# Dividing layer 0's softmax rows before the turn, a token-tile last step in layer 2, and one pool of tiles

## The chip, the cores and the metric

One core of one Trainium2 chip. The metric is device time in microseconds (us), the median of the runs. The kernel before takes 4326.4 us (4324.36 to 4327.26); the prediction starts from 4325.7 us, one of these runs. Runs of one kernel agree within 0.2%, so differences of 10 us are read as real where three rounds were timed.

## The reference, cut to what matters

64 graphs of 256 nodes with 256 features pass through four layers, each added to its input after a layer norm and a ReLU. Only layers 0 and 2 change.

```python
# layer 0: 8 heads of 32, masked softmax over keys
scores = einsum('bhqd,bhkd->bhqk', q, k) / sqrt(32)
w = softmax(where(adj > 0, scores, -1e9), axis=-1)
ctx = einsum('bhqk,bhkd->bhqd', w, v)            # then @ Wo + bo
# layer 2: three GRU steps, the adjacency passing messages
for i in range(3):
    aggr = einsum('bst,bsd->btd', A, h @ weight[i])
    r = sigmoid(i_r + h_r); z = sigmoid(i_z + h_z)
    n = tanh(i_n + r * h_n)
    h = (1 - z) * n + z * h
```

Layer 1 is a graph attention, layer 3 one with four heads.

## The kernel before

Two graphs make a pair, 32 pairs in all. Every piece of work is a task: one or more forms (engine, assumed duration, instructions), what it reads, writes and claims. A list scheduler in the kernel orders all tasks beforehand from the assumed durations, picking at each step the task and form that can begin first. The result is one fixed queue for each engine; on the chip each queue runs strictly in that order.

```python
def evict(n, dst, src):                      # an eviction: copy a result out of PSUM; either engine may do it
    return [(A, act(n), lambda: nc.scalar.copy(dst(), src())),
            (V, dve(n), lambda: nc.vector.tensor_copy(dst(), src()))]
def dve2(n):
    return 0.065 + n / 1920.0
def pool(n):
    return 0.16 + n / 460.0

SLOTS = {...
    "w4": (20, [P, T * D], FP, 6),           # count, shape, type, reserve for the oldest pair
    "w8": (4, [P, 8, N], FP, 1),
    "w2": (5, [P, N2], FP, 2), "rzw": (4, [P, 2, 4, D0], FP, 2), ...}
```

In layer 0 the exponentials of a row are turned (transposed on TensorE) undivided. The reciprocals of the row sums are widened to 32 columns a head, turned as well, and multiply the context.

```python
add(exp_group(s, mx, zs, rows, ...), reads=[(mx, half)], writes=[s, (zs, half)])
for k in range(2):
    add((PE, 4 * TURN, turn), reads=[s], writes=[ps], claims=[pT[half]])
    add(evict(N2, ...), reads=[ps], writes=[(pT[half], (ti, k))])
# ... after both tiles of the graph:
add((V, 0.2, reciprocal(rz, zs)));  add((V, 0.22, copy(rzw, rz widened)))
add((PE, 4 * TURN, turn_rz), reads=rzws, writes=[psz])      # four transposes
add((A, act(N2), copy(rzT, psz)))
add((PE, 1.93, context), ...)
add((V, dve(N2), cT = psc * rzT))
```

In layer 2 each gate is computed with features along the partitions, so that its bias rides on ScalarE's activation; each step ends with eight transposes back to tokens.

```python
ps = gate(3.44, ((whhT, hT), (giT[:, l], aT)), o * P, o)     # 4 fp32 products of 512 columns
add((A, act(N2, 1), tanh(r, ps, bias=brz[:, o:o+1], scale=0.5)))
# ... u = 0.5 * (z' + 1) * (h - n) + n
add((PE, 4 * TURN, tokens), reads=[hT], writes=[ps])          # twice
add_to_x(xt, g, ps)                                           # last step: VectorE, out of PSUM
```

## Time and profile before

| | kernel before |
|---|---|
| median | 4326.4 us |
| TensorE, VectorE, ScalarE, GpSimd busy | 98%, 68%, 53%, 14% |
| one pair of graphs, in the periodic part | 132.47 us |

How the page and the start distances are read stands in the prediction. What TensorE waited for between 1000 and 4200 us (total, times, longest) is little:

```profile
PE ps L930 <- ACT w L401: 8.7, 8, 1.1
PE ps L909 <- DVE w L402: 5.7, 7, 0.8
PE ps L840 <- DVE w L828: 4.7, 8, 0.6
```

GpSimd's timeline during the slow VectorE group that the prediction shows (2065.72 us, 3.62 us for four operations):

```profile
2065.04 1.27 POOL L811 TENSOR_TENSOR w<-w,w 128x512 f32<-128x512 f32 x1 [9.81 <-ACT w L806]
2066.64 1.27 POOL L811 TENSOR_TENSOR w<-w,w 128x512 f32<-128x512 f32 x1 [0.32 <-ACT w L806]
2067.88 1.31 POOL L506 TENSOR_TENSOR x<-x,bo_bc 128x512 f32<-128x512 f32 x1
2069.41 1.75 POOL L506 TENSOR_TENSOR x<-x,bo_bc 128x512 f32<-128x512 f32 x1 [0.23 <-DVE w L445]
```

### The profile page before, as it was taken

Reading aid. Unit: us, or ns where it says so; the run is one execution under the profiler, and the core shown is the slowest. Engines: PE = TensorE matmul, PEld = TensorE weight load, DVE = VectorE, ACT = ScalarE, POOL = GpSimd, SP = SyncE. Lnnn points to the kernel's source line nnn. Section 1 sums busy time; section 2 is a strip of 40 time slices with the busy share of each in tenths; the row PEclk is TensorE's granted clock in tenths of the full one; section 3 lists DMA queues with packets and bytes.
Section 4 is the critical chain, followed back from the end, with each engine's and each line's share of the span. In section 5 each row is a group of like instructions: output and inputs, shape, how many; then the busy total and the mean of one; then the engine's idle time right before and its main releaser. Section 6 shows DMA issues by size and latency. Waiting matters only on the chain.

```text
span 4324.5 us, 56216 instructions
## 1 busy us (share of the span) xinstructions
PE 4244.1 (98%) x20720; PEld 2631.3 (61%) x20720; DVE 2930.0 (68%) x5426; ACT 2301.1 (53%) x6105; POOL 590.3 (14%) x582
## 2 busy tenths in 40 slices
PE   7999999999999999999999999999999999999997
PEld 5665566656656665666566566656655665666564
DVE  6775577667657755876676577558765765776554
ACT  4664465545545644655455456446554554564444
POOL 1111111111111111111111111111111111111111
PEclk9999999999999999999999999999999999999999
DMA  2000011000000000010000000000100100000000
GB/s 83 21 18 22 20 36 34 20 16 24 30 25 25 13 28 25 30 35 20 11 30 30 25 25 13 27 25 26 40 11 17 32 30 25 25 13 28 15 15 15
DMA packets 109986, 108.47 MB, mean 25 GB/s; under 512 B 7312, under 2 KB 109712, under 8 KB 109712
## 3 DMA queue, kind: packets, MB, share of 16 engines
q1 hardware_dynamic: 109712, 104.89, 7.6%
q8 instruction: 163, 2.67, 0.3%
q14 instruction: 111, 0.91, 0.1%
HBM read 88.09 MB, written 16.78 MB: 24 GB/s over the span
## 4 chain that ended last, share of the span: by engine, by line
PE 77%; DVE 8%; issue 8%; ACT 5%; POOL 1%; SPq 0%; DMA 0%; POOLq 0%; ACTq 0%; DVEq 0%
PE ps L761 36%; PE ps L775 7%; PE ps L518 5%; PE ps L480 5%; PE ps L573 4%; PE ps L717 3%; PE ps L654 3%; PE ps L540 2%; PE ps L457 2%; PE ps L614 2%; PE ps L840 2%; PE ps L858 2%; ACT w L886 2%; ACT w L494 2%; DVE w L823 1%
## 5 line engine op out<-in xcount | busy, mean ns | idle before, releaser
L761 PE MATMUL ps<-w,whhT 128*128 128x512 f32 x2304 | 1080.3, 595 | 0.7 <-DVE w L402 0.4
L761 PE MATMUL ps<-w,giT 128*128 128x512 f32 x2304 | 1063.6, 593 | 0.0
L494 ACT ACTIVATE w<-w,mx 128x256 f32<-128x256 f32 x1664 | 825.7, 503 | 186.3 <-DVE mx L561 128.9
L401 ACT COPY w<-ps 128x512 f32<-128x512 f32 x983 | 553.0, 587 | 657.3 <-PE ps L775 290.8
L761 PEld LDWEIGHTS ps<-w,giT 128*128 128x128 f32 x2304 | 433.6, 190 | 523.9 <-issue 513.3
L761 PEld LDWEIGHTS ps<-w,whhT 128*128 128x128 f32 x2304 | 415.3, 190 | 406.6 <-issue 383.9
L811 POOL TENSOR_TENSOR w<-w,w 128x512 f32<-128x512 f32 x192 | 251.2, 1317 | 1689.6 <-ACT w L806 1331.8
L402 DVE COPY w<-ps 128x512 f32<-128x512 f32 x553 | 366.4, 684 | 153.7 <-PE ps L573 58.0
L786 ACT ACTIVATE w<-ps,brz 128x512 f32<-128x512 f32 x192 | 131.8, 687 | 463.2 <-PE ps L761 460.3
L791 DVE TENSOR_SCALAR w<-w 128x512 f32<-128x512 f32 x192 | 81.6, 425 | 407.8 <-ACT w L786 407.7
L554 DVE SCALAR_TENSOR_TENSOR w<-ps,mask 128x512 f32<-128x512 f32 x512 | 333.3, 680 | 33.9 <-PE ps L540 33.9
L775 PE MATMUL ps<-w,w 128*128 128x256 f32 x1536 | 355.7, 379 | 0.0
L775 PEld LDWEIGHTS ps<-w,w 128*128 128x128 f32 x1536 | 286.2, 190 | 60.7 <-issue 22.9
L494 ACT ACTIVATION_READ_ACCUMULATOR w<-w,mx 128x1 f32 x1664 | 322.9, 194 | 0.0
L823 DVE SCALAR_TENSOR_TENSOR w<-w,w 128x512 f32<-128x512 f32 x192 | 152.5, 794 | 246.3 <-ACT w L818 240.7
L561 DVE TENSOR_REDUCE mx<-w 128x4 f32<-128x1024 f32 x256 | 309.2, 1208 | 2.0
L573 PE MATMUL ps<-ident,w 128*128 128x128 f32 x2048 | 269.4, 273 | 0.6
L573 PEld LDWEIGHTS ps<-ident,w 128*128 128x128 f32 x2048 | 235.1, 140 | 57.1 <-issue 25.6
L818 ACT ACTIVATE w<-ps,brz 128x512 f32<-128x512 f32 x192 | 130.8, 681 | 235.0 <-PE ps L761 234.9
L424 POOL TENSOR_SCALAR rs<-mv 128x4 f32<-128x4 f32 x128 | 33.6, 262 | 1354.8 <-DVE mv L417 1293.5
L886 ACT ACTIVATE w<-w,f 128x256 f32<-128x256 f32 x512 | 217.1, 503 | 1.4
L445 DVE TENSOR_SCALAR w<-x,mv,rs 128x256 f32<-128x256 f32 x384 | 185.3, 541 | 16.5 <-POOL rs L425 15.8
(113 smaller groups left out, 5633.0 us busy)
## 6 DMA issues: line engine op xcount, KB each, us to landing
adj<-in_adj_dram SPq DMA_DIRECT2D x128, 512.0 KB, 4.1
x<-in_x_dram SPq DMA_DIRECT2D x64, 256.0 KB, 2.8
out_dram<-x SPq DMA_DIRECT2D x64, 256.0 KB, 2.2
gg_sb<-in_L_gnn_weight_dram SPq DMA_DIRECT2D x3, 256.0 KB, 3.7
wih_sb<-in_L_gnn_w_ih_dram SPq DMA_DIRECT2D x1, 768.0 KB, 6.9
whh_sb<-in_L_gnn_w_hh_dram SPq DMA_DIRECT2D x1, 768.0 KB, 8.6
wq_sb<-in_L_gnn_Wq_dram SPq DMA_DIRECT2D x1, 256.0 KB, 2.8
wk_sb<-in_L_gnn_Wk_dram SPq DMA_DIRECT2D x1, 256.0 KB, 3.0
```

What stands on the lines that cost most here:

```text
L401: (A, act(n), lambda: nc.scalar.copy(dst(), src())),
L402: (V, dve(n), lambda: nc.vector.tensor_copy(dst(), src())),
L480: mm(ps()[:, c * D : (c + 1) * D], chunk(src, k, 2 * g + c), rhs[:, k, :], start=k == 0, stop=k == 1)
L494: nc.scalar.activation(tok(e(), N)[:, i, :], tok(e(), N)[:, i, :], AF.Exp, bias=mx()[:, m : m + 1], accum_out=zs()[:, z : z + 1],)
L518: mm(ps(), w[:, k, o * P : (o + 1) * P], tok(hT(), N2)[:, k, :], start=k == 0, stop=k == 1)
L554: (V, dve(N2), lambda s=s, j=j, b=b, t=t: nc.vector.scalar_tensor_tensor(tok(s(), N)[:, 2 * j : 2 * j + 2, :], tok(b(), N), SCALE, tok(mb( ...
L561: (V, dve(4 * N), lambda s=s, mx=mx, h4=h4: nc.vector.tensor_reduce(mx()[:, h4], tok(s(), N), AX.X, ALU.max, negate=True)),
L573: nc.tensor.transpose(tok(ps(), P)[:, 2 * i + c, :], tok(s(), N)[:, 2 * k + i, c * P : (c + 1) * P], ident,)
L761: mm(ps(), w[:, k, c0 : c0 + P], at_o(src, k), start=n == 0, stop=n == 2 * len(terms) - 1)
L775: mm(ps()[:, g * N : (g + 1) * N], tok(h())[:, t, o * P : (o + 1) * P], tok(am(), N)[:, t, :], start=c == 0, stop=c == 1,)
L811: (G, pool(N2), lambda o=o, u=u, hT=hT, hn=hn: nc.gpsimd.tensor_sub(at_o(u, o), at_o(hT, o), at_o(hn, o))),
L886: (A, act(N, 1), lambda t=t, g=g, h=h, e=e: nc.scalar.activation(tok(e(), N)[:, h, :], tok(sd[h // 2](), N2)[:, h % 2, g * N : (g + 1) * N ...
```

## The change

The intent is to take transposes off TensorE, the busiest engine: the row division moves ahead of the turn, so the reciprocals need no turn of their own; layer 2's last step gives token tiles (tokens along the partitions) at once. The tiles of 8 KB become pairs of 4 KB from one pool.

```diff
-        "w4": (20, [P, T * D], FP, 6),
-        "w8": (4, [P, 8, N], FP, 1),
+        "w4": (28, [P, T * D], FP, 9),
-        "w2": (5, [P, N2], FP, 2),
+        "w2": (4, [P, N2], FP, 2),
-        "rzw": (4, [P, 2, 4, D0], FP, 2),
+    row_bcast(brz_bc, b_ih[0:N2])          # and bhn_bc, bhh_bc: biases along the free axis
# layer 0, per tile and half
+    add((V, 0.13, rz = 1 / zs), reads=[(zs, half)], writes=[(rz, half)])
     for k in range(2):
+        add([(V, 2 * dve2(N), divided),     # two tensor_scalar of 128x256 with a pointer scalar
+             (G, pool(N2), lambda ...: nc.gpsimd.tensor_tensor(two(), two(),
+                 rz()[:, z0 : z0 + 2].unsqueeze(2).to_broadcast([P, 2, N]), ALU.mult))],
+            reads=[(rz, half)], writes=[(s, k)])
-        add((PE, 4 * TURN, turn), reads=[s], writes=[ps], claims=[pT[half]])
+        add((PE, 4 * TURN, turn), reads=[(s, k)], writes=[ps], claims=[pT[2 * half + k]])
-    add((V, 0.22, widen rz)); add((PE, 4 * TURN, turn_rz)); add((A, act(N2), copy rzT))
-    add((V, dve(N2), cT = psc * rzT))
+    add(evict(N2, cT, psc))
# layer 2, last step: token chunks stationary, weights moving
+    add((PE, 3.44, tokens_mm(ps, both, t, 0, N2)))                      # r and z of a chunk
+    add((V, dve(N2), rz[g] = ps + brz_bc)); add((A, act(N2), tanh(rz[g], scale=0.5)))
+    add((V, ..., hn = (r + 1) * hn)); add((V, ..., hn = 0.5 * hn + ps))
+    add((V, ..., hn += bias));        add((A, act(N2), tanh(hn)))
+    add((G, pool(N2), h = h - hn));   add((G, pool(N2), x = x + hn))
+    add((V, ..., h = (z + 1) * h));   add((V, ..., x = 0.5 * h + x))
-    add((PE, 4 * TURN, tokens)); add_to_x(xt, g, ps)                    # last step only
# ... cut: layer 3's eT from the same pool, the moved helper for the messages
```

More of the change, by code (lines that the diff above doesn't have):

```diff
@@ L266, in tile_adj_preln_d4 @@
     nc.sync.dma_start(bhh_sb, b_hh.rearrange("(k p) -> p k", p=P))
+    brz_bc = const.tile([P, N2], FP, name="brz_bc")
+    bhn_bc = const.tile([P, 2, D], FP, name="bhn_bc")
+    row_bcast(brz_bc, b_ih[0:N2])
+    row_bcast(bhn_bc[:, 0], b_ih[N2 : 3 * D])
+    row_bcast(bhn_bc[:, 1], b_hh[N2 : 3 * D])
     with tc.tile_pool(name="prep", bufs=1) as prep:
@@ L283, in transposed @@
                     nc.vector.tensor_copy(dst[:, k, o * P : (o + m) * P], ps[:, 0 : m * P])
+        bhh_bc = prep.tile([P, N2], FP, name="bhh_bc")
+        row_bcast(bhh_bc, b_hh[0:N2])
+        nc.vector.tensor_add(brz_bc, brz_bc, bhh_bc)
         gg_sb = prep.tile([P, NL, 2, D], FP, name="gg_sb")
@@ L528, in layer0 @@
         for g in range(2):
-            pT = [buf("w8") for half in range(2)]
-            rzws = []
+            pT = [w4() for i in range(4)]
             for ti in range(2):
@@ L533, in layer0 @@
                 banks, ss = [bank() for hh in range(4)], [w4() for half in range(2)]
-                zs, mx = buf("zs"), buf("mx")
+                zs, mx, rz = buf("zs"), buf("mx"), buf("rz")
                 def scores(t=t, g=g, banks=banks):
@@ L546, in scores @@
                             )
-                add((PE, 1.11, scores), reads=[qT, kT], writes=banks, claims=[*ss, zs, mx])
+                add((PE, 1.11, scores), reads=[qT, kT], writes=banks, claims=[*ss, zs, mx, rz])
                 for half in range(2):
@@ L566, in layer0, with divided @@
                     add(exp_group(s, mx, zs, rows, f"0_{p}_{t}"), reads=[(mx, half)], writes=[s, (zs, half)])
+                    add(
+                        (V, 0.13, lambda rz=rz, zs=zs, h4=h4: nc.vector.reciprocal(rz()[:, h4], zs()[:, h4])),
+                        reads=[(zs, half)], writes=[(rz, half)],
+                    )
                     for k in range(2):
                         ps = bank()
+                        def divided(s=s, k=k, half=half, rz=rz):
+                            for i in (2 * k, 2 * k + 1):
+                                z = 4 * half + i
+                                nc.vector.tensor_scalar_mul(tok(s(), N)[:, i, :], tok(s(), N)[:, i, :], rz()[:, z : z + 1])
+                        two = lambda s=s, k=k: tok(s(), N)[:, 2 * k : 2 * k + 2, :]
+                        z0 = 4 * half + 2 * k
+                        add(
+                            [
+                                (V, 2 * dve2(N), divided),
+                                (G, pool(N2), lambda two=two, z0=z0, rz=rz: nc.gpsimd.tensor_tensor(
+                                    two(), two(), rz()[:, z0 : z0 + 2].unsqueeze(2).to_broadcast([P, 2, N]), ALU.mult)),
+                            ],
+                            reads=[(rz, half)], writes=[(s, k)],
+                        )
                         def turn(s=s, k=k, ps=ps):
@@ L581, in layer0 @@
                                 N2,
-                                lambda half=half, k=k, ti=ti, pT=pT: pT[half]()[:, 4 * k : 4 * k + 4, ti * P : (ti + 1) * P],
+                                lambda dst=pT[2 * half + k], ti=ti: tok(dst(), N)[:, :, ti * P : (ti + 1) * P],
                                 lambda ps=ps: tok(ps(), P),
                             ),
-                            reads=[ps], writes=[(pT[half], (ti, k))],
+                            reads=[ps], writes=[(pT[2 * half + k], ti)],
                         )
-                rz, rzw = buf("rz"), buf("rzw")
-                add((V, 0.2, lambda rz=rz, zs=zs: nc.vector.reciprocal(rz(), zs())), reads=[zs], writes=[rz])
-                add(
-                    (V, 0.22, lambda rz=rz, rzw=rzw: nc.vector.tensor_copy(
-                        rzw(), rz().rearrange("p (h c) -> p c h", c=2).unsqueeze(3).to_broadcast([P, 2, 4, D0]))),
-                    reads=[rz], writes=[rzw],
-                )
-                rzws.append(rzw)
-            psz, rzT = bank(), buf("w2")
-            def turn_rz(psz=psz, rzws=rzws):
-                for ti in range(2):
-                    for cc in range(2):
-                        nc.tensor.transpose(
-                            psz()[:, cc * N + ti * P : cc * N + (ti + 1) * P],
-                            rzws[ti]()[:, cc].rearrange("p h d -> p (h d)"), ident,
-                        )
-            add((PE, 4 * TURN, turn_rz), reads=rzws, writes=[psz], claims=[rzT])
-            add((A, act(N2), lambda rzT=rzT, psz=psz: nc.scalar.copy(rzT(), psz())), reads=[psz], writes=[rzT])
             psc = bank()
@@ L616, in context @@
                                 tok(v())[:, 2 * g + c, h * D0 : (h + 1) * D0],
-                                pT[hh // 2]()[:, 4 * (hh % 2) + 2 * cc + c, :],
+                                tok(pT[hh](), N)[:, 2 * cc + c, :],
                                 start=c == 0,
@@ L623, in layer0 @@
             add(
-                (V, dve(N2), lambda g=g, psc=psc, rzT=rzT: nc.vector.tensor_tensor(
-                    tok(cT(), N2)[:, :, g * N : (g + 1) * N], tok(psc(), N), tok(rzT(), N), ALU.mult)),
-                reads=[psc, rzT], writes=[(cT, g)],
+                evict(N2, lambda g=g: tok(cT(), N2)[:, :, g * N : (g + 1) * N], lambda psc=psc: tok(psc(), N)),
+                reads=[psc], writes=[(cT, g)],
             )
@@ L747, in layer2, with messages, product @@
         add((V, dve2(T * N), lambda: nc.vector.tensor_scalar(am(), at(), 0.0, None, ALU.not_equal)), reads=[at, hT], writes=[am])
-        for l in range(NL):
-            nm = f"{p}_{l}"
+        at_o = lambda b, o: tok(b(), N2)[:, o, :]
+        def messages(h):
             aT = w4()
+            for o in range(2):
+                ps = bank()
+                def product(o=o, ps=ps):
+                    for g in range(2):
+                        for c in range(2):
+                            t = 2 * g + c
+                            mm(
+                                ps()[:, g * N : (g + 1) * N], tok(h())[:, t, o * P : (o + 1) * P], tok(am(), N)[:, t, :],
+                                start=c == 0, stop=c == 1,
+                            )
+                add((PE, 1.73, product), reads=[h, am], writes=[ps], claims=[aT])
+                add(evict(N2, lambda o=o: at_o(aT, o), ps), reads=[ps], writes=[(aT, o)])
+            return aT
+        for l in range(NL - 1):
             r, hn, u = w4(), w4(), w4()
-            at_o = lambda b, o: tok(b(), N2)[:, o, :]
             def gate(us, terms, c0, o, claims=()):
@@ L767, in layer2 @@
             pshn = [gate(1.72, ((whhT, hT),), (4 + o) * P, o, [r, hn]) for o in range(2)]
-            for o in range(2):
-                ps = bank()
-                def messages(o=o, ps=ps, h=h):
-                    for g in range(2):
-                        for c in range(2):
-                            t = 2 * g + c
-                            mm(
-                                ps()[:, g * N : (g + 1) * N], tok(h())[:, t, o * P : (o + 1) * P], tok(am(), N)[:, t, :],
-                                start=c == 0, stop=c == 1,
-                            )
-                add((PE, 1.73, messages), reads=[h, am], writes=[ps], claims=[aT])
-                add(evict(N2, lambda o=o, aT=aT: at_o(aT, o), ps), reads=[ps], writes=[(aT, o)])
+            aT = messages(h)
             both = ((whhT, hT), (giT[:, l], aT))
@@ L832, in layer2 @@
             hT = u
-            h = w4() if l < NL - 1 else None
+            h = w4()
             for g in range(2):
@@ L840, in tokens @@
                             nc.tensor.transpose(ps()[:, c * D + k * P : c * D + (k + 1) * P], chunk(hT, k, 2 * g + c), ident)
-                add((PE, 4 * TURN, tokens), reads=[hT], writes=[ps], claims=[h] if h else [])
-                if h is None:
-                    add_to_x(xt, g, ps)
-                else:
-                    add(evict(N2, lambda g=g, h=h: h()[:, g * N2 : (g + 1) * N2], ps), reads=[ps], writes=[(h, g)])
+                add((PE, 4 * TURN, tokens), reads=[hT], writes=[ps], claims=[h])
@@ new lines, in layer2, with tokens_mm @@
+                add(evict(N2, lambda g=g, h=h: h()[:, g * N2 : (g + 1) * N2], ps), reads=[ps], writes=[(h, g)])
+        l, rz, hn = NL - 1, [w4() for g in range(2)], w4()
+        two = lambda ap, g: tok(ap())[:, 2 * g : 2 * g + 2, :]
+        bias = lambda i: bhn_bc[:, i : i + 1, :].to_broadcast([P, 2, D])
+        def tokens_mm(out, terms, t, c0, n):
+            m = 0
+            for w, src in terms:
+                for k in range(2):
+                    mm(out, chunk(src, k, t), w[:, k, c0 : c0 + n], start=m == 0, stop=m == 2 * len(terms) - 1)
+                    m += 1
@@ new lines, in new_gate, with product @@
+        def new_gate(w, src, g, claims=()):
+            ps = bank()
+            def product():
+                for c in range(2):
+                    tokens_mm(ps()[:, c * D : (c + 1) * D], ((w, src),), 2 * g + c, N2, D)
+            add((PE, 1.74, product), reads=[src], writes=[ps], claims=claims)
+            return ps
+        for g in range(2):
+            ps = new_gate(whhT, hT, g, [hn])
+            add(
+                (V, dve(N2), lambda g=g, ps=ps: nc.vector.tensor_tensor(two(hn, g), tok(ps()), bias(1), ALU.add)),
+                reads=[ps], writes=[(hn, g)],
+            )
@@ new lines, in layer2 @@
+        aT = messages(h)
+        both = ((whhT, hT), (giT[:, l], aT))
+        for g in range(2):
+            for c in range(2):
+                ps = bank()
+                add(
+                    (PE, 3.44, lambda t=2 * g + c, ps=ps: tokens_mm(ps(), both, t, 0, N2)),
+                    reads=[hT, aT], writes=[ps], claims=[rz[g]],
+                )
+                add(
+                    (V, dve(N2), lambda g=g, c=c, ps=ps: nc.vector.tensor_tensor(at_o(rz[g], c), ps(), brz_bc, ALU.add)),
+                    reads=[ps], writes=[(rz[g], c)],
+                )
+                add(
+                    (A, act(N2), lambda g=g, c=c: nc.scalar.activation(at_o(rz[g], c), at_o(rz[g], c), AF.Tanh, scale=0.5)),
+                    writes=[(rz[g], c)],
+                )
+            gate_of = lambda g, i: tok(rz[g](), N2)[:, :, i * D : (i + 1) * D]
+            add(
+                (V, dve(N2), lambda g=g, gate_of=gate_of: nc.vector.scalar_tensor_tensor(
+                    two(hn, g), gate_of(g, 0), 1.0, two(hn, g), ALU.add, ALU.mult)),
+                reads=[rz[g]], writes=[(hn, g)],
+            )
+            ps = new_gate(giT[:, l], aT, g)
+            add(
+                (V, dve(N2), lambda g=g, ps=ps: nc.vector.scalar_tensor_tensor(
+                    two(hn, g), two(hn, g), 0.5, tok(ps()), ALU.mult, ALU.add)),
+                reads=[ps], writes=[(hn, g)],
+            )
+            add(
+                (V, dve(N2), lambda g=g: nc.vector.tensor_tensor(two(hn, g), two(hn, g), bias(0), ALU.add)),
+                writes=[(hn, g)],
+            )
+            add((A, act(N2), lambda g=g: nc.scalar.activation(two(hn, g), two(hn, g), AF.Tanh)), writes=[(hn, g)])
+            add((G, pool(N2), lambda g=g: nc.gpsimd.tensor_sub(two(h, g), two(h, g), two(hn, g))), reads=[(hn, g)], writes=[(h, g)])
+            add((G, pool(N2), lambda g=g: nc.gpsimd.tensor_add(two(xt, g), two(xt, g), two(hn, g))), reads=[(hn, g)], writes=[(xt, g)])
+            add(
+                (V, dve(N2), lambda g=g, gate_of=gate_of: nc.vector.scalar_tensor_tensor(
+                    two(h, g), gate_of(g, 1), 1.0, two(h, g), ALU.add, ALU.mult)),
+                reads=[rz[g]], writes=[(h, g)],
+            )
+            add(
+                (V, dve(N2), lambda g=g: nc.vector.scalar_tensor_tensor(
+                    two(xt, g), two(h, g), 0.5, two(xt, g), ALU.mult, ALU.add)),
+                reads=[(h, g)], writes=[(xt, g)],
+            )
@@ L879, in layer3 @@
             zs, rz = buf("zs"), buf("rz")
-            eT = buf("w8")
+            eT = [w4() for k in range(2)]
             for ti in range(2):
@@ L911, in turn @@
                                 )
-                    add((PE, 4 * TURN, turn), reads=[e], writes=[ps], claims=[eT])
+                    add((PE, 4 * TURN, turn), reads=[e], writes=[ps], claims=[eT[k]])
                     add(
@@ L916, in layer3 @@
                             N2,
-                            lambda k=k, ti=ti, eT=eT: eT()[:, 4 * k : 4 * k + 4, ti * P : (ti + 1) * P],
+                            lambda dst=eT[k], ti=ti: tok(dst(), N)[:, :, ti * P : (ti + 1) * P],
                             lambda ps=ps: tok(ps(), P),
                         ),
-                        reads=[ps], writes=[(eT, (ti, k))],
+                        reads=[ps], writes=[(eT[k], ti)],
                     )
@@ L932, in product @@
                                 f()[:, 2 * g + c, h * C3 : (h + 1) * C3],
-                                eT()[:, 2 * h + c, :],
+                                tok(eT[k](), N)[:, 2 * j + c, :],
                                 start=c == 0,
@@ L936, in product @@
                             )
-            add((PE, 1.86, product), reads=[eT, (f, 2 * g), (f, 2 * g + 1)], writes=[pso], claims=[oT])
+            add((PE, 1.86, product), reads=[*eT, (f, 2 * g), (f, 2 * g + 1)], writes=[pso], claims=[oT])
             add(evict(N2, oT, pso), reads=[pso], writes=[oT])
```

## The prediction

> **What bounds the kernel now.** I read the page's busy shares and its row of 40 slices first, then the busy time of each engine over three stretches of equal length, then TensorE's timeline over one pair of graphs, then the list of what TensorE waited for, and last the two ends of the run.
>
> ```profile
> PE 4244.1 (98%) x20720; PEld 2631.3 (61%) x20720; DVE 2930.0 (68%) x5426; ACT 2301.1 (53%) x6105; POOL 590.3 (14%) x582
> ...
> PE   7999999999999999999999999999999999999997
> ```
>
> TensorE is busy from the second slice to the second last. A busy TensorE need not be at its peak, so I looked for a period. The chain of waits repeats every 397.4 us (1180.57, 1577.98, 1975.40, 2372.80), in which TensorE runs 1933 matmul passes each time. All 32 pairs run 20720 passes with the preparation, about 645 a pair, so 397.4 us is three pairs, 132.47 us each. Columns below: window, its length, TensorE, weight loads, VectorE, ScalarE, GpSimd, each with its count.
>
> ```profile
> 1180.57:1577.98 397.41, 394.37 (x1933) 244.63 (x1933) 274.60 (x507) 215.13 (x571) 55.20 (x54) 1.00 0.08 25
> 1577.98:1975.40 397.42, 394.38 (x1933) 244.65 (x1933) 274.52 (x507) 215.12 (x571) 55.23 (x54) 1.00 0.08 25
> ```
>
> Per pair: TensorE 131.5 of 132.5 us busy, VectorE 91.5, ScalarE 71.7, GpSimd 18.4. The order of instructions is fixed beforehand by a list scheduler that mixes layers 0, 1 and 3 of neighbouring pairs into layer 2, which explains the exact repetition. So the time is 32 pairs of 132.47 us (4239 us) and 86 us of both ends. What takes a microsecond of TensorE work out of a pair takes about 32 us off; what adds work elsewhere costs nothing until an engine's queue runs late.
>
> The unit cost of TensorE work is a distance between starts, since durations overlap. Columns: start, duration, engine, line.
>
> ```profile
> 2013.21 0.60 PE L600 MATMUL ps<-ident,rzw 128*128 128x128 f32 x4
> 2013.74 1.93 PE L614 MATMUL ps<-w,w 128*32 128x256 f32 x32
> ...
> 2077.81 1.04 PE L840 MATMUL ps<-ident,w 128*128 128x128 f32 x8
> 2078.69 3.60 PE L761 MATMUL ps<-w,whhT 128*128 128x512 f32 x8
> 2082.12 5.34 PE L775 MATMUL ps<-w,w 128*128 128x256 f32 x24
> 2087.30 1.88 PE L761 MATMUL ps<-w,whhT 128*128 128x512 f32 x4
> 2089.02 1.88 PE L761 MATMUL ps<-w,giT 128*128 128x512 f32 x4
> ...
> 2135.16 0.60 PE L600 MATMUL ps<-ident,rzw 128*128 128x128 f32 x4
> 2135.60 1.88 PE L761 MATMUL ps<-w,whhT 128*128 128x512 f32 x4
> ```
>
> Eight passes of the turn to tokens (L840) take 0.88 us, four of the turn of the reciprocals (L600) 0.53 or 0.44 us, a pass of 512 columns 0.429 us (3.43 / 8), one of 256 columns 0.216 us (5.18 / 24). Each fp32 product shows as two passes, a transpose as one.
>
> **What the Trainium skill says.** (1) "Perfetto Trace Analysis", section "Identifying the Most-Contended Engine": matmul busy time is a poor measure of closeness to the roofline, as pipelined instructions look smaller. I agree and use start distances; the trace bears it out (1.04 us shown for 0.88 us of work). (2) "TensorE: Matmul & The Clock Gate", "LDWEIGHTS (loading the stationary operand)": the load's time follows its columns. Here a 128-column fp32 load takes 190 ns, under the 216 ns of a 256-column pass, so the new gates with twice the loads should stay hidden; the 256-wide messages (L775) already do. (3) "SBUF — State Buffer", "Who interferes with whom": VectorE in a two-port mode, or with two SBUF inputs, and GpSimd block each other for a whole instruction. The trace agrees:
>
> ```profile
> 2002.61 1.38 DVE L445 TENSOR_SCALAR w<-x,mv,rs 128x256 f32<-128x256 f32 x4 [0.37 <-POOL rs L425]
> ...
> 2065.72 3.62 DVE L445 TENSOR_SCALAR w<-x,mv,rs 128x256 f32<-128x256 f32 x4
> ```
>
> The same four operations take 1.38 us with GpSimd idle and 3.62 us while it runs four 512-wide operations from 2065.04 to 2071.16 (GpSimd timeline).
>
> **The change, part by part.**
>
> Layer 0, TensorE: the eight passes a pair that turn the widened reciprocals go. Two groups at 0.44 to 0.53 us: minus 0.97 us on average of the two sightings. The turns of the exponentials and the context products keep their number and shape.
>
> Layer 0, others: gone are per pair four reciprocals (0.198 us each), four widening copies (0.350), two multiplies of the context (0.682) on VectorE, 3.6 us, and two ScalarE copies (0.586). New are eight smaller reciprocals (about 0.17, between the 0.159 of 128x2 and the 0.198 of 128x8): 1.4 us; two plain evictions of the context, which I give one to each engine (0.68 and 0.59); and 16 divides of 128x512. On VectorE a divide is two 128x256 operations with a pointer scalar; L445 is of that kind, 0.541 us mean with collisions, so 1.08 us. On GpSimd it is one operation with a broadcast input, like L506 at 1.407 us. The scheduler takes whichever engine can begin first; VectorE is 69% busy and GpSimd 14%, so I guess half and half: 8.7 us on VectorE, 11.3 us on GpSimd.
>
> Layer 2, last step, TensorE: its eight passes of turning to tokens go, minus 0.88 us. The r and z gates keep four products of 512 columns for each of four results: the stationary side is now the token chunk and the moving side the weights, 3.43 us each as before. The four n gates become eight passes of 256 columns, 1.73 us, where they were four of 512, 1.717 us: plus 0.05 us for four.
>
> Layer 2, VectorE: the old step has per half 0.425 + 0.747 + 0.682 + 0.794 + 0.736 + the addition to x 0.684 = 4.07 us. The bias now runs along the free axis, so it can no longer ride on ScalarE's activation: per graph three additions out of PSUM (0.68 each), one fused operation out of PSUM (0.68), and four with two SBUF inputs (0.79 each, as L823) = 5.88 us. Twice the difference: plus 3.6 us. ScalarE keeps six tanh. GpSimd gets two more additions (1.317): plus 2.6 us.
>
> Sum per pair: TensorE minus 0.97 minus 0.88 plus 0.05 = minus 1.80 us. VectorE minus 3.6 plus 1.4 plus 0.7 plus 8.7 plus 3.6 = plus 10.8, to 102 us of some 130.7 (78%). ScalarE about 71. GpSimd plus 13.9, to 32 (25%). TensorE stays the bound, so the period falls to about 130.7 us and 32 pairs give minus 57.6 us.
>
> The pool: four tiles of 8 KB and twenty of 4 KB become 28 of 4 KB, the same room, given out in finer parts. TensorE's waits name no full pool; the largest inside the periodic part are for evictions. I book nothing for it.
>
> The ends, where nothing hides:
>
> ```profile
> 15.96 2.79 PE L278 MATMUL ps<-ident,wih_sb 128*128 128x128 f32 x12 [15.96 <-DMA wih_sb<-in_L_gnn_w_ih_dram]
> ...
> 4281.57 0.27 PE L840 MATMUL ps<-ident,w 128*128 128x128 f32 x1
> 4284.03 0.98 PE L840 MATMUL ps<-ident,w 128*128 128x128 f32 x7 [2.19 <-DVE w L828]
> 4284.62 1.29 DVE L634 TENSOR_TENSOR x<-ps,x 128x512 f32<-128x512 f32 x2 [0.64 <-PE ps L840]
> ```
>
> At the start four loads (256, 128, 128 and 256 KB) are put ahead of the weights that TensorE waits for. About 3 MB lands in the 15 us before that wait ends, 0.2 MB/us, and each issue takes 0.5 us: estimate plus 3 us. At the end, the old step takes 4.3 us from the last gate to the new x. The new one has, from the last r/z product: add 0.7, tanh 0.65, three VectorE operations 1.9, tanh 0.65, GpSimd 1.27, two VectorE operations 1.3, with some 0.2 us of hop at each change of engine, about 8 us, of which the last n gate covers 1.7 and the earlier statistics of the first graph give back about 0.9. Estimate plus 1.5 us, once.
>
> Sum: 4325.7 - 57.6 + 3 + 1.5 = 4272.6, rounded to 4273 us.
>
> **The rivals.** (a) VectorE becomes late. GpSimd's busy time rises by three quarters, layer 0's own stretch has VectorE at 78% already (103.26 of 132 us in the window 564 to 696), and each divide now stands between exponential and turn. For it: the 3.62 us above, and a widening copy that once took 1.178 us against a median of 0.293. Against it: TensorE's visible wait for another engine between 1000 and 4200 us is only 22 us in all. At 0.3 to 1 us more waiting per pair the result is 4283 to 4305. (b) The schedule gets better. The turn to tokens waited for VectorE 13 times (11.3 us, 4.7 of it in the periodic part), some of that goes, and the finer pool lets the scheduler fill the other gaps: TensorE idles 3.0 us of each 397.4 (32 us over the run), and the distances between starts hide a few more. If half of that goes: 4250 to 4258. (c) The transposes only filled time in which TensorE would have waited, and nothing comes of taking them out: 4320 to 4330. TensorE's idle share of 0.8% speaks against it.
>
> **Range and chances.** The central step is arithmetic on the bound engine, and its error is small (0.44 or 0.53 us: plus or minus 3 us). The spread comes from the new order of instructions, which I can't see: 18 us better by (b), 25 us worse by (a). 8 times in 10 between 4253 and 4298 us. Faster by over 2% needs 4239 us, 34 us beyond my sum, more than all visible idle time: 0.05. Within 2%: 0.92. Slower by over 2%: 0.03, only with VectorE as the bound.
>
> **What would show each step.** A period of about 392 us for three pairs with 1885 passes, TensorE still at 98 to 99%; VectorE near 306 us and GpSimd near 95 us in it; TensorE's first wait near 19 us; ScalarE unchanged. Wrong if divides fall nearly all on one engine, if TensorE's waits for the turn of the exponentials grow by tens of microseconds, or if the gaps between passes of the token gates exceed 0.22 and 0.43 us because their weight loads now wait for fresh data.

## The result, and the profile after

The changed kernel takes 4396.8 us (4394.69 to 4403.02), a ratio of 1.0166 (1.0148 to 1.0183). The prediction of 4273 us, with 4253 to 4298 us as its range, is missed by 124 us and on the wrong side.

Engine totals, then two stretches of three pairs each (the pattern now repeats after 403.3 us):

```profile
PE 4239.4 (96%) x20720; PEld 2671.8 (61%) x20720; DVE 3262.6 (74%) x5996; ACT 2277.1 (52%) x6096; POOL 960.5 (22%) x910
```

```profile
1568.57:1971.89 403.32, 394.30 (x1934) 248.21 (x1933) 305.90 (x560) 212.14 (x569) 89.89 (x85) 1.00 0.08 25
1971.89:2375.12 403.23, 394.26 (x1934) 248.15 (x1933) 306.15 (x560) 212.03 (x569) 90.47 (x85) 1.00 0.08 24
```

The work is what was predicted: VectorE 306 us per three pairs (predicted 306), GpSimd 90 (95), ScalarE nearly unchanged (212, before 215). Yet the period grew from 397.4 to 403.3 us where it should have fallen to 392. TensorE shows 9.0 us of idle time in it, before 3.0. Per pair the time is 134.4 us, against 132.47 less 1.8 us of removed work: TensorE waits some 3.7 us more per pair. Only 2.0 us of that is visible as idle time. The rest must lie inside what is shown as busy, where ends are modelled: the best version below shows some 388 us of busy time for as many passes, this kernel 394.

TensorE's waits between 1000 and 4200 us name the place: L599 is the turn of layer 0's exponentials, L583 the divide on VectorE, L722 a product of layer 1, L712 layer 1's scaling.

```profile
PE ps L599 <- DVE w L583: 31.6, 44, 1.7
PE ps L722 <- DVE w L712: 13.0, 6, 2.2
```

The groups (count, busy, mean ns, idle time before): a divide on GpSimd, half a divide on VectorE, and layer 2's h = (z + 1) * h on VectorE.

```profile
L590 POOL TENSOR_TENSOR w<-w,rz 128x512 f32<-128x512 f32 x264 | 285.0, 1083 | 1075.2 <-DVE rz L574 998.9 <-PE ps L546 24.5 <-PE ps L722 20.2
L583 DVE TENSOR_SCALAR w<-w,rz 128x256 f32<-128x256 f32 x496 | 278.5, 604 | 3.2
L920 DVE SCALAR_TENSOR_TENSOR w<-w,w 128x512 f32<-128x512 f32 x64 | 96.0, 1500 | 40.4 <-POOL w L917 40.4
```

The scheduler did split the divides in half (248 and 264). The last line is the striking one: 1500 ns in the mean for an operation that takes 690 elsewhere. A piece of the timeline of all engines shows both faults:

```profile
2047.77 1.27 POOL L918 TENSOR_TENSOR x<-x,w 128x512 f32<-128x512 f32 x1
2047.85 1.74 DVE L920 SCALAR_TENSOR_TENSOR w<-w,w 128x512 f32<-128x512 f32 x1 [0.33 <-POOL w L917]
...
2051.88 0.17 DVE L574 RECIPROCAL rz<-zs 128x4 f32<-128x4 f32 x1
...
2052.08 1.50 DVE L583 TENSOR_SCALAR w<-w,rz 128x256 f32<-128x256 f32 x2
2052.12 1.04 POOL L590 TENSOR_TENSOR w<-w,rz 128x512 f32<-128x512 f32 x1 [3.09 <-DVE rz L574]
...
2053.37 0.70 PE L599 MATMUL ps<-ident,w 128*128 128x128 f32 x4 [1.64 <-DVE w L583]
```

At 2047.77 GpSimd starts its addition to x. VectorE's next operation starts 0.08 us later and ends only after GpSimd's has. At 2051.88 one reciprocal releases a divide on VectorE and one on GpSimd at once; GpSimd's begins 40 ns after VectorE's first and ends at 2053.16. VectorE's first takes 1.23 us and ends only after that, its second 0.34 us, so two operations of a third of a microsecond take 1.50 us. TensorE's next turn waits 1.64 us. The Trainium skill, "SBUF — State Buffer", "Who interferes with whom", says that the port pair the two engines share is an exclusive lock for a whole instruction; this trace agrees, in that VectorE's operation outlasts GpSimd's both times, at 2052.08 even with the earlier start.

The token gates themselves behave as predicted: 1.72 us for four passes of 512 columns, 1.73 us for eight of 256 (distances between starts).

```profile
2019.22 1.89 PE L863 MATMUL ps<-whhT,w 128*128 128x256 f32 x8
2020.95 1.89 PE L764 MATMUL ps<-w,w 128*128 128x256 f32 x8
...
2030.47 1.88 PE L863 MATMUL ps<-whhT,w 128*128 128x512 f32 x4
2032.19 1.88 PE L863 MATMUL ps<-giT,w 128*128 128x512 f32 x4
```

One thing the study passes over is TensorE's granted clock. Its mean over the span (`--cores`) is 0.996 before and 0.991 after. An estimate from these: 0.4% of 4324.5 us is 17 us, 0.9% of 4395.3 us is 40 us, so up to some 22 us of the 70 us lost lie in stretches of lower clock. Those shown above read 1.00, but the one from 425 to 450 us reads 0.80 (before 0.93). Whether the lower clock follows from the waits or adds to them was not tested. The mean is known to 0.001, which is 4 us.

### The profile page after: what moved, and what is told of

The parts are those of the page before. It is cut to its first block, busy times and chain, and to the rows that moved or that the text cites. A ratio compares the mean times of both kernels' runs of the same rounds, so it can differ in the third digit from the quotient of the medians.

```text
span 4395.3 us, 56915 instructions
## 1 busy us (share of the span) xinstructions
PE 4239.4 (96%) x20720; PEld 2671.8 (61%) x20720; DVE 3262.6 (74%) x5996; ACT 2277.1 (52%) x6096; POOL 960.5 (22%) x910
## 4 chain that ended last, share of the span: by engine, by line
PE 62%; DVE 31%; ACT 5%; issue 2%; POOL 1%; DMA 0%; SPq 0%; POOLq 0%; DVEq 0%; ACTq 0%
PE ps L783 20%; PE ps L863 7%; PE ps L764 6%; DVE mx L567 5%; DVE w L560 5%; PE ps L525 5%; PE ps L487 4%; DVE w L583 4%; DVE w L409 3%; PE ps L1012 2%; PE ps L722 2%; PE ps L620 2%; PE ps L599 2%; PE ps L464 2%; ACT w L501 2%; DVE w L974 2%
## 5 line engine op out<-in xcount | busy, mean ns | idle before, releaser
L783 PE MATMUL ps<-w,whhT 128*128 128x512 f32 x1536 | 725.4, 597 | 2.2 <-ACT w L408 1.7
L783 PE MATMUL ps<-w,giT 128*128 128x512 f32 x1536 | 720.3, 594 | 5.3 <-ACT w L795 4.3
L590 POOL TENSOR_TENSOR w<-w,rz 128x512 f32<-128x512 f32 x264 | 285.0, 1083 | 1075.2 <-DVE rz L574 998.9
L783 PEld LDWEIGHTS ps<-w,giT 128*128 128x128 f32 x1536 | 284.7, 190 | 332.9 <-issue 321.3
L863 PE MATMUL ps<-whhT,w 128*128 128x512 f32 (+1 forms) x1024 | 363.9, 489 | 0.0
L863 PE MATMUL ps<-giT,w 128*128 128x512 f32 (+1 forms) x1024 | 356.7, 486 | 0.0
L599 PE MATMUL ps<-ident,w 128*128 128x128 f32 x2048 | 282.4, 277 | 44.5 <-DVE w L583 39.5
L599 PEld LDWEIGHTS ps<-ident,w 128*128 128x128 f32 x2048 | 231.2, 141 | 138.3 <-DVE w L583 58.1
L863 PEld LDWEIGHTS ps<-giT,w 128*128 128x128 f32 x1024 | 192.1, 190 | 148.7 <-issue 137.8
L583 DVE TENSOR_SCALAR w<-w,rz 128x256 f32<-128x256 f32 x496 | 278.5, 604 | 3.2
L795 ACT ACTIVATE w<-ps,brz 128x512 f32<-128x512 f32 x128 | 87.8, 686 | 318.6 <-PE ps L783 318.6
L863 PEld LDWEIGHTS ps<-whhT,w 128*128 128x128 f32 x1024 | 186.1, 190 | 102.0 <-issue 86.2
```

What stands on the lines that cost most here:

```text
L583: nc.vector.tensor_scalar_mul(tok(s(), N)[:, i, :], tok(s(), N)[:, i, :], rz()[:, z : z + 1])
L590: (G, pool(N2), lambda two=two, z0=z0, rz=rz: nc.gpsimd.tensor_tensor(two(), two(), rz()[:, z0 : z0 + 2].unsqueeze(2).to_broadcast([P, 2, ...
L599: nc.tensor.transpose(tok(ps(), P)[:, 2 * i + c, :], tok(s(), N)[:, 2 * k + i, c * P : (c + 1) * P], ident,)
L783: mm(ps(), w[:, k, c0 : c0 + P], at_o(src, k), start=n == 0, stop=n == 2 * len(terms) - 1)
L863: mm(out, chunk(src, k, t), w[:, k, c0 : c0 + n], start=m == 0, stop=m == 2 * len(terms) - 1)
```

## The experiments

Theory A: VectorE and GpSimd block each other at the divides, and the turns wait. A2: so does GpSimd's addition to x. B: the pool, or layer 2's gates, cost the time. C: VectorE simply has too much work. D: the path through a divide is too long. E: the scheduler's order is at fault. Eighteen runs, all with three rounds.

### One part at a time

A control comes first, since layer 2's step alone does not fit beside the old buffers.

```diff
# c0_small_buffers: kernel before
-        "w2": (5, ...), "rzw": (4, ..., 2)
+        "w2": (4, ...), "rzw": (3, ..., 1)
# e1_layer0_only: kernel before + the divides, pT still from "w8"
# e2_layer2_only: c0 + layer 2's last step
# e3_pool_only:   kernel before + "w4": (28, ..., 9), pT and eT from it
```

> Control for the next run: the kernel before with one 2 KB tile fewer and three instead of four tiles for the widened reciprocals (the layer-2 step alone does not fit otherwise). Every theory: within 10 us of the kernel before, 4316 to 4336 us. If it is further off, the layer-2 run is read against this one.

Measured 4326.1 us, 0.9997 (0.9981 to 1.0014). The smaller buffers cost nothing.

> Only layer 0's divides, old pools, old layer 2. TensorE's work falls by 0.97 us a pair (31 us). Theory A, VectorE and GpSimd block each other at the divides and the turns wait: the turns lose about 2 us a pair (what the changed kernel's start distances show), so 4355 to 4370 us. Theory B, the pool or layer 2 is to blame: 4290 to 4305 us. Theory C, VectorE has simply too much work: in between, 4320 to 4340 us, as only two thirds of the added work is here.

Measured 4422.9 us, 1.0222 (1.0207 to 1.0237): the direction of theory A, but 53 us beyond its range.

> Only layer 2's last step in token tiles, layer 0 and pools as before (with the control's smaller buffers). TensorE's work falls by 0.83 us a pair (27 us). Theory A (the loss sits at layer 0's divides): 4300 to 4315 us. Theory A2 (GpSimd's addition to x blocks VectorE for 1 us at each graph here too, and what follows on VectorE is late): 4330 to 4350 us. Theory B with layer 2's gates waiting for their weight loads: over 4340 us, with the token gates' passes more than 0.43 and 0.22 us apart.

Measured 4344.5 us, 1.0040 (1.0025 to 1.0055): in A2's range. The token gates' passes lie 0.22 and 0.43 us apart in the median, as predicted, so B's waiting gates fall. But the mean clock fell too, to 0.991, which by the estimate above is worth up to some 22 us. This run alone doesn't show A2; run f2 below tests it.

> Only the pool: 28 tiles of 4 KB in place of 20 and four of 8 KB. No work changes. Theories A and C: within 10 us of the kernel before, 4316 to 4336 us. Theory B for the pool: 4345 us or more, by a worse order of instructions.

Measured 4339.8 us, 1.0030 (1.0015 to 1.0044): between the two expectations.

Every part alone costs time, by 96, 17 and 13 us against the kernel before in the same rounds (4327.3 us). Their sum is 125 us, but the whole costs 70. The parts do not add up; the fixed order, which differs in each, may be why.

### Which engine divides

```diff
 add([
-    (V, 2 * dve2(N), divided),
-    (G, pool(N2), ...nc.gpsimd.tensor_tensor...),
+    (V, 2 * dve2(N), divided),                 # e4_divide_vector
+    (G, pool(N2), ...),                        # e5_divide_gpsimd
+    (A, 1.0, divided with nc.scalar.mul),      # e6_divide_scalar
 ])
# e7_xadd_vector: the x = x + hn of layer 2's last step
-    add((G, pool(N2), nc.gpsimd.tensor_add(x, x, hn)))
+    add((V, dve(N2), nc.vector.tensor_tensor(x, x, hn, ALU.add)))
```

> The changed kernel with every divide of layer 0 on VectorE (two pointer operations of about 0.33 us each) and none on GpSimd. VectorE gets some 5 us a pair more, GpSimd 8 us less. Theory A (collisions on the shared port at the divides): better than the changed kernel by 30 us or more, 4340 to 4367 us, and the divides' mean falls from 604 ns to about 400. Theory C (VectorE has too much work): worse than it, 4400 to 4450 us.

Measured 4363.3 us, 1.0084 (1.0069 to 1.0099). All divides on VectorE, none on GpSimd, and 33 us better than the changed kernel; the mean of half a divide falls from 604 to 364 ns. Theory C said worse and falls as the main cause.

> The changed kernel with every divide on GpSimd (1.04 us each) and none on VectorE. VectorE loses 8.7 us a pair. Theory A: GpSimd's own divides no longer start beside VectorE's, but 16 us a pair of GpSimd work still block VectorE's other two-input operations: 4370 to 4420 us. Theory C: 4330 to 4360 us, as VectorE is back at 70%.

Measured 4369.5 us, 1.0098 (1.0083 to 1.0113): 0.5 us below A's range, 9.5 us above C's, so nearer to A without deciding it.

> The changed kernel with every divide on ScalarE (two multiplications by a pointer scalar of 128x256, some 0.5 us each, 16 us a pair; ScalarE goes from 71 to about 86 us of 130)[...]. Both A and C: 4300 to 4345 us, the first version that could beat the kernel before. If it is over 4380 us, neither the port nor VectorE's load is the cause, but the longer path from exponential to turn itself (theory D).

Measured 4309.7 us, 0.9961 (0.9946 to 0.9976). On ScalarE every half of a divide takes 491 to 555 ns, so nothing holds it up; 87 us are gone and the kernel before is beaten by 17. A and C both allowed this. Theory D falls for this order of instructions.

> The changed kernel with the addition of the new state to x (layer 2's last step) on VectorE in place of GpSimd. In the changed kernel GpSimd runs it at the very moment VectorE needs the port for the next operation, which then takes 1.50 us instead of 0.69. Theory A2: that blocked microsecond costs more than the 0.6 us of added VectorE work, so 4380 to 4392 us, 5 to 15 us better. Theory C: 5 to 10 us worse.

Measured 4430.0 us, 1.0242 (1.0225 to 1.0259): 33 us worse where I expected better. The blocked operation did fall to 687 ns, and TensorE's largest wait became one of layer 2's gates for evictions by ScalarE (69.1 us). The edit changed the whole order, so it tests two things at once. The next runs hold the order fixed.

### The same order, a cost taken away

These give wrong results. Only the number of columns of one operation is cut to 8, so every engine's queue has the same instructions in the same order. The mean clocks of these four runs and of the changed kernel are 0.991 to 0.992, so the clock doesn't separate them.

```diff
# f1: two() -> two()[:, :, 0:8] in GpSimd's divide
# f2: x[:, :, 0:8] += hn[:, :, 0:8] in GpSimd's addition to x
# f3: tok(s(), N)[:, i, 0:8] in VectorE's divide
# f4: all three
# e8_true_cost (right result, new order): the scheduler's assumption
-    (V, 2 * dve2(N), divided),
+    (V, 0.75, divided),
```

> The changed kernel with the very same order of instructions on every engine, but GpSimd's 264 divides cut to 8 of 256 columns (a wrong result on purpose), so that they hold the shared port for a moment only. VectorE's own work is untouched. Theory A (port collisions at the divides): VectorE's divides fall from a mean of 604 ns to below 400 and the time by 25 us or more, to under 4372 us. Theory C (VectorE's load) or E (the order of instructions alone): 4385 to 4397 us.

Measured 4316.1 us, 0.9976 (0.9961 to 0.9990): 81 us less than the changed kernel, with no column of VectorE's work removed. VectorE's divides, of the same size as before:

```profile
L583 DVE TENSOR_SCALAR w<-w,rz 128x256 f32<-128x256 f32 x496 | 170.8, 388 | 3.2
```

And what TensorE's queue for these turns waited for, weight loads included (us, times), first in the changed kernel:

```profile
  DVE w L583: 97.7, 121
  issue: 57.9, 179
  POOL w L590: 8.0, 19
```

then in this run (loads and products wait side by side, so a sum is not time lost):

```profile
  issue: 51.8, 179
  DVE w L583: 16.5, 25
```

The turns hardly ever waited for GpSimd's own results (8.0 us). They waited for VectorE's, and VectorE was held up by GpSimd.

> The changed kernel in the same order of instructions, with GpSimd's addition to x in layer 2's last step cut to 8 of 256 columns (wrong result on purpose). The last run with this addition on VectorE came out 33 us slower, against my expectation, but its order had changed. Theory A2 (that addition blocks VectorE for 1 us a graph): the operation after it falls from 1500 to under 800 ns and the time by 8 to 25 us, to 4372 to 4389 us. Otherwise within 5 us of the changed kernel.

Measured 4382.8 us, 1.0127 (1.0112 to 1.0142): 14 us for the addition's collision, as A2 said; the blocked operation's mean fell from 1500 to 686 ns.

> The changed kernel in the same order, with VectorE's 496 divides cut to 8 of 256 columns (wrong result on purpose) and GpSimd's left whole. VectorE loses some 5 to 8 us of work a pair, and its divides hardly collide any more. Theory A or C: both say faster, C by more than the GpSimd cut (over 30 us), A by about as much. Theory E (order alone): within 10 us of the changed kernel.

Measured 4357.2 us, 1.0068 (1.0053 to 1.0083): 40 us less, half of what f1 gave, where theory C said more than f1. The group line is the neatest evidence:

```profile
L583 DVE TENSOR_SCALAR w<-w,rz 128x8 f32<-128x8 f32 x496 | 216.1, 482 | 3.2
```

An operation of eight columns takes 482 ns in the mean. With GpSimd's divides cut too (f4, below) the same one takes:

```profile
L583 DVE TENSOR_SCALAR w<-w,rz 128x8 f32<-128x8 f32 x496 | 103.7, 257 | 3.2
```

Some 225 ns of the mean go with GpSimd's columns: they were waiting, by theory A for the port.

> The changed kernel, with nothing changed but the duration that the scheduler assumes for a divide on VectorE: 0.75 us in place of 0.40 (measured: two at 0.33 between starts, 604 ns mean with collisions). Theory E (an order laid out for divides that are too short): the time falls by 20 us or more, to under 4377 us. Theory A: more divides move to GpSimd, the collisions stay, 4370 to 4410 us.

Measured 4379.9 us, 1.0122 (1.0105 to 1.0139): 17 us better, inside A's range and 3 us outside E's; the mean of half a divide is 629 ns, so the collisions stay. A truer assumed duration helps a little; it knows nothing of collisions.

### What is left

```diff
# g1_layer0_scalar: e1 with the divides on ScalarE
# g3_pool_spare6:   e3 with reserve 6 in place of 9
# g2_scalar_x_last: e6, and in layer 2's last step
-    add((G, ..., x = x + hn))
     add((V, ..., h = (z + 1) * h))
-    add((V, ..., x = 0.5 * h + x))
+    add((V, ..., hn = 0.5 * h + hn))
+    add((G, ..., x = x + hn))
# h1_x_last_old_divides: the changed kernel with that last step
# h2_layer2_x_last:      e2 with that last step
```

> The changed kernel in the same order of instructions, with GpSimd's divides, VectorE's divides and GpSimd's addition to x all cut to 8 columns (wrong result on purpose): the removed TensorE work without the added cost. If collisions and VectorE's divides are all that stands between the prediction and the result: 4268 to 4285 us. If the order of instructions costs something of its own: 4290 to 4310 us.

Measured 4306.3 us, 0.9951 (0.9937 to 0.9966). Without both collisions and VectorE's divides, 91 us of the 124 us miss are explained in this order; some 33 us are not. The mean clock is 0.992: up to some 17 us of the 33 lie in stretches of lower clock.

> The kernel before with only layer 0 changed and its divides on ScalarE; old layer 2, old pools. TensorE loses 0.97 us a pair, 31 us. If what TensorE loses comes off the time once no port is in the way: 4290 to 4305 us. If layer 0's path is too long with a divide in it: 4320 us or more.

Measured 4361.3 us, 1.0079 (1.0064 to 1.0094), a miss. It is 62 us better than the same kernel with the split divides (4422.9), so ScalarE helps here too, but 34 us over the kernel before. The largest wait of TensorE is now layer 3's turn, for exponentials on ScalarE:

```profile
PE ps L905 <- ACT w L494: 44.0, 20, 5.3
```

The expectation gave 4320 us or more to theory D, but the longest list of TensorE's waits has only 0.6 us for layer 0's turns, so the longer path in layer 0 is not what shows. Why this order makes layer 3 wait stays open; it fits ScalarE's higher load (60% busy), which no run separates from the order. The mean clock of 0.990 alone is worth up to some 26 us.

> The changed kernel with the divides on ScalarE (4310 us so far), and in layer 2's last step the addition to x on GpSimd moved behind the last VectorE operation, so that VectorE's operation of 1.6 us falls to 0.7 us. Theory A2: 4288 to 4303 us. If the new order undoes it, as with the addition on VectorE: 4310 us or more.

Measured 4258.8 us, 0.9842 (0.9827 to 0.9856), with a right result: the best version, 1.6% faster than the kernel before and better than expected. The operation h = (z + 1) * h, blocked before (min, median, max ns), and all engines in two stretches of three pairs' length:

```profile
L917 DVE SCALAR_TENSOR_TENSOR w<-w,w x64: 679/684/694, 276.3 to 4216.0; 128x512 f32<-128x512 f32 x64
```

```profile
1500.00:1889.20 389.20, 388.63 (x2001) 250.24 (x1998) 286.47 (x542) 253.14 (x686) 61.61 (x59) 1.00 0.08 25
1889.20:2278.40 389.20, 388.06 (x1869) 246.64 (x1869) 274.08 (x515) 230.19 (x620) 64.60 (x61) 1.00 0.08 26
```

TensorE is idle for less than 0.3%, and the distance between the starts of layer 3 in the 7th and the 25th pair is 2335.2 us, 129.73 us a pair. The predicted 130.7 us a pair was attainable.

> The pool alone once more, with the reserve of tiles kept for the oldest pair at 6 in place of 9; no instruction differs from the pool-alone run but their order. If the order alone moves the time by as much as the pool run lost (13 us): anywhere from 4315 to 4345 us, and different from 4340 by 5 us or more. If the common pool itself costs the 13 us: 4337 to 4343 us.

Measured 4341.0 us, 1.0031 (1.0014 to 1.0048), 1 us from the pool's other run. The reserve doesn't matter; the pool's 13 us stand in both orders. In the run with 9, TensorE's waits between 300 and 4200 us are nearly all of one kind:

```profile
PE ps L908 <- DVE w L401: 47.8, 55, 1.6
```

That is layer 3's turn behind an eviction on VectorE (the same wait in the kernel before: 6.9 us). Whether the pool or the order near it is the cause is not settled.

> The changed kernel (divides on VectorE or GpSimd) with the addition to x placed last. Theory A: the divides' collisions return, so it stays far above the version with ScalarE's divides: 4340 to 4390 us. If the place of the addition and the order it leads to were the whole matter: under 4290 us.

Measured 4595.2 us, 1.0623 (1.0605 to 1.0641), far outside both expectations and the slowest of all. The divides on both engines are back, but their collisions do not explain 200 us: the largest waits are for layer 3's norm and exponentials.

```profile
PE ps L464 <- DVE w L452: 98.8, 12, 9.8
PE ps L991 <- ACT w L501: 77.9, 25, 6.0
```

Here pairs follow each other with bare stretches, 9.8 us at once, as at the end of the run: the order no longer lays one pair's layers 0, 1 and 3 under another's layer 2. The mean clock there is 0.972, by the estimate worth up to some 89 us of the 198 us over the changed kernel. A bad order, in other words, from moving one addition.

> The kernel before with only layer 2's last step changed and its addition to x placed last (with the control's smaller buffers; with the addition in its old place 4345 us). If the step's saving of TensorE work comes through once the collision is gone: 4300 to 4315 us. If the order of instructions decides instead: anything from 4320 to 4350 us.

Measured 4372.8 us, 1.0108 (1.0093 to 1.0123): 28 us worse than with the addition in its old place, a miss. The trace shows why in part: in the new order a different VectorE operation, layer 1's scaling, meets GpSimd's (min, median, max ns), and TensorE waits 58.3 us for it (L726, 27 times).

```profile
L716 DVE TENSOR_TENSOR w<-w,rz x64: 678/1432/1787, 131.7 to 4109.7; 128x512 f32<-128x512 f32 x64
```

The scaling's mean was 785 ns in e2 and is 1499 ns here, while the operations beside the addition fell to some 685 ns. The collision was not removed but moved. An order that repeats with every pair repeats such a meeting in every pair.

## Why the prediction was wrong, point by point

**What bounds the kernel.** Right as far as it went: the removed TensorE work is real. Distances between starts agree with the sum (1.72 and 1.73 us), and the best version reaches 129.73 us a pair. TensorE's busy total falls from 4244.1 to 4185.7 us there, 58.4 us where the prediction has 57.6. (The prediction takes from the Trainium skill, "Perfetto Trace Analysis", "Identifying the Most-Contended Engine", that pipelined matmuls look smaller in a trace; the groups here look longer, 1.04 us shown for 0.88 us between starts. The starts are the right measure either way.) The idea that what adds work elsewhere "costs nothing until an engine's queue runs late" was the wrong test. A queue can be late locally at 74% busy.

**Work on the other engines.** VectorE was predicted to the microsecond, in part by luck: the operation at L920 alone took 1.4 us a pair more than its term, so other terms were too large. GpSimd came within 5 us of 95 per three pairs, and the divides' half and half split, a guess, was right. A divide on GpSimd took 1.08 us, not 1.41; a pair of VectorE operations 1.21, not 1.08.

**The step that failed** is the one that says "TensorE stays the bound, so the period falls to about 130.7 us"; it rose to 134.4. I priced collisions as VectorE busy time, by the mean of another line (L445, 0.541 us), and not as delay in front of the turns. Two things were missed. One reciprocal releases both engines' divides, so they meet by construction. And GpSimd's two operations in layer 2 stand directly ahead of the VectorE operation that needs the port; I added their 1.3 us to GpSimd's total and 0.79 us for VectorE's, where the mean came to 1.50. In the same order of instructions the first is worth 81 us and the second 14 us; with VectorE's divides cut as well it is 91 us in all, so the effects overlap.

**Rival (a)** named this mechanism, from the right lines, and was mis-sized: "0.3 to 1 us more waiting per pair" was 3.7 us in the result.

**Rival (b)**, that a better order would gain, did not happen. **Rival (c)** falls with the best version.

**The ends.** First wait at 18.7 us, predicted near 19. From the last gate to the new x it took 7.2 us against 4.3, of which the collision is 1.0; less the prediction's 0.9 us for earlier statistics of the first graph, the net is about 2 us (an estimate), predicted 1.5.

**The pool**, booked at nothing, costs 13 us alone. **The range** gave 25 us for a worse order; runs with hardly other work lie from 4259 to 4595 us. "1885 passes" was a slip: the n gates' doubled passes make up for the transposes removed, and 1934 were counted.

**Open:** 33 us of the miss in the changed kernel's own order (up to some 17 of them at lower clock), why g1 and the pool cost what they do, and how much of the 51 us from e6 to g2 is order; the collision it removes was worth 14 us in another order, and the mean clock rose from 0.992 to 0.995, up to some 13 us.

## What to carry to other kernels

Before giving work to "whichever of VectorE and GpSimd is free", ask whether both will touch SBUF at the same moment: the port they share makes two short operations into one long wait, and the sum of busy times does not show it. Try such work on ScalarE if it has room; here it gained in both orders tested (87 and 62 us), though in g1 not enough to beat the kernel before. When a fixed order comes out of a list scheduler, test a cause by cutting an operation's size with the order held, because any edit that changes the order can move the time by more than the effect you look for. Compare the mean granted clocks as well.

## What the Trainium skill lacked or had wrong

- "SBUF — State Buffer", "Who interferes with whom": the lock is stated and right, its size for small operations is not. An eight-column VectorE operation beside GpSimd's divides took 482 ns in the mean, 257 without them; one of 512 columns with two SBUF inputs took 1500 instead of 690 ns.
- "GPSIMD Engine Reference", section 3.1 "Elementwise — side-by-side cycle accounting": the two-input figure has no case for a broadcast operand. The divide with a reciprocal broadcast along 256 columns took 1.04 us at 128x512 (median), two full inputs 1.27 us.
- "TensorE: Matmul & The Clock Gate", "LDWEIGHTS (loading the stationary operand)": columns divided by 1.2 GHz gives 107 ns for 128 columns. That fits the bf16 loads here (98 ns), but fp32 loads took 190 ns, and 140 ns ahead of fp32 transposes.
- No page treats what these runs showed at large: a statically ordered kernel where small edits moved the time from 4259 to 4595 us.
